# An expert's last rows as one step of 32, 64 or 96 rows: the expert loop of a graph network with a mixture of experts

## The chip, the cores and the metric

The kernel runs on one core of a Trainium2 chip. The metric is device time in microseconds, the median of several runs. The profile beside it is one execution of the same program, taken by the hardware profiler; its span runs from the first instruction to the last.

## The reference

The input is a graph of 625 nodes with 768 features each and 20,000 edges. Two layers of graph attention come first, then a transformer block whose feed-forward part is a mixture of eight experts, all in float32. Every node goes to the one expert with the largest gate value (`K = 1`, so its weight is 1):

```python
gate_logits = h2 @ Wg                                   # h2: 625 x 768, Wg: 768 x 8
w, sel = jax.lax.top_k(gate_logits, 1)
hid = relu(einsum('nd,edf->enf', h2, W1) + b1)          # W1: 8 x 768 x 3072
y = einsum('enf,efd->end', hid, W2) + b2                # W2: 8 x 3072 x 768
out = x + einsum('ne,end->nd', combine, y)              # combine: one 1 in each row
```

The reference computes every expert for every node and keeps one. The kernel computes each node's own expert alone. How many nodes an expert gets is known only when the gate has run.

## The kernel before, in words

**Before the experts.** The graph layers and the attention take the first 640 us. As each block of 125 nodes leaves the attention, `gate` and `choose` find its experts, and `send` scatters its rows into two DRAM buffers, `xg` (what the expert reads) and `xr` (what the result is added to), sorted by expert: an expert has 640 places (`RE`).

**The first expert.** The expert that most nodes of the first block chose is loaded early; up to 128 of its rows are worked on as `step_a` while the last blocks are still being sent.

**The step table.** Meanwhile VectorE works out, on one partition, what is left to do (L1194 to L1294). It sorts the experts by size, splits each one's rows into steps and fills a table with one column for each step: expert, whether its weights are new, kind of step (0: 128 rows, 1: 64, 2: 32) and first row. An expert's rows are rounded up to a multiple of 32; the multiple of 128 in them gives steps of 128, and what is left (0, 32, 64 or 96) a step of 32, one of 64, or one of each. Within an expert the step of 32 comes first, then that of 64, then those of 128. The table has room for `NS` = 20 steps; the intermediate arrays have 20 x 8 = 160 elements.

**The loop over steps** (L1321 to L1340). In each turn GpSimd gathers the next step's rows into `xb` (L1328) and this step's sums so far into `rb` (L1046); then `tc.If` chooses one of three bodies, `step(128)`, `step(64)` or `step(32)`. The code of each body stands in the program once on every engine.

**A step of M rows** has P = 128 / M groups. The stationary operand of a matmul is then only M columns wide, and P of them stand side by side in the tensor engine and in PSUM, each with another slice of the weights. W1 and W2 each lie in SBUF in three pieces of 3 MB (`w1[c]`, `w2[c]`), each loaded in two halves. A step of 32 or 64 rows takes a piece at a time:

- `into(c)` (L1074): rows times piece c of W1 into the PSUM tile `ph`, and VectorE copies that to `hb` (L1083).
- `turn(c)` (L1086): TensorE turns `hb` (L1090); ScalarE adds the bias, takes the ReLU and writes `hbT` (L1095).
- `out_of(c)` (L1097): `hbT` times piece c of W2, summed over all c in the PSUM tile `py` (L1102).

The order on TensorE is written out (L1130 to L1141): all `into` with the `turn`s between them, then all `out_of`; among the last two of these the next step's rows are turned (`turn_rows`, L879). At the end VectorE adds `py`, group by group, to `yo`, which holds the sums so far and the bias `b2` (L1149 to L1154), and GpSimd scatters `yo` to the output (L1156).

**The weights.** There is one set of buffers. After each step's code SyncE has `load_expert` (L1054) for the next step: six halves of W1 (L1025), the bias block `b2b` (L1031), six halves of W2 (L1019). Each is issued when the current step no longer reads what it overwrites. All issues carry a condition: where the next step has the same expert, they are passed over and no byte is moved.

## Time and profile before

| | |
|---|---|
| median of 3 runs | 1089.4 us (1086.68 to 1089.96) |
| the profiled execution: time | 1088.95 us |
| its span | 1086.4 us |
| PE busy | 1012.5 us, 93% of the span |
| VectorE, ScalarE, GpSimd busy | 450.8, 318.8, 57.9 us |
| mean granted TensorE clock | 0.978 |
| `step_a` on PE | from 642.3 |
| nine steps of the loop on PE | 714.5 to 1073.7 |

The page names engines PE (matmuls), PEld (weight loads into the array, beside PE), DVE (VectorE), ACT (ScalarE), POOL (GpSimd) and SP (SyncE); a q behind the name is the engine's sequencer, which waits, branches and issues transfers. "L1102" is a line of the kernel. A float32 matmul of the program shows as two records. In a group's line the bar is followed by its busy time, the mean ns of one, and the idle time of the engine before it with what ended that. The chain of waits follows the work back from the last instruction, at each step to what released it.

PE's share of 93% is a mean over stages with different limits: the attention and the graph layers are not touched by this change, and in the loop the share differs from step to step.

### The profile page before, as it was taken

What the parts mean: (1) busy time and instruction counts of PE and PEld (TensorE: products, weight loads), DVE (VectorE), ACT (ScalarE), POOL (GpSimd) and SP (SyncE); (2) the same over time, 40 slices, a digit from 0 to 9 for tenths busy, and PEclk for the clock granted to TensorE, in tenths of its full rate; (3) what the DMA queues carried; (4) which work ended last, traced back from release to release, by engine and by line L of the source; (5) the groups of instructions that cost most, each with busy time, mean ns of one, the idle gap of its engine ahead of it and who ended that gap; (6) DMA issues with size and microseconds to landing.
All of it is one profiled execution on the core that took longest, in us unless ns stands there. A gap on an engine that the chain in (4) does not pass through costs nothing. (4 is left out here: it accounts for less than half of the span.)

```text
span 1086.4 us, 14453 instructions
## 1 busy us (share of the span) xinstructions
PE 1012.5 (93%) x4763; PEld 578.2 (53%) x4764; DVE 450.8 (41%) x1264; ACT 318.8 (29%) x820; POOL 57.9 (5%) x97
## 2 busy tenths in 40 slices
PE   6889799999989989999999999999999889998993
PEld 4455366677555556666765655544454435533341
DVE  6796776385174740465546655011101121011211
ACT  6677534362140020344443401110201112021120
POOL 1200100000000100000000111000000000000000
PEclk9999899999999999999999999999999899998997
DMA  9300400300430164999200759111799948899694
GB/s 287 121 1 1 157 1 0 131 1 19 102 97 1 51 125 80 404 377 342 76 1 3 288 176 373 59 46 37 274 325 381 403 179 325 297 406 403 244 405 159
DMA packets 85669, 194.48 MB, mean 179 GB/s; under 512 B 32397, under 2 KB 34068, under 8 KB 85609
## 3 DMA queue, kind: packets, MB, share of 16 engines
q1 hardware_dynamic: 79817, 174.00, 44.9%
q0 software_dynamic: 5712, 19.54, 5.1%
q8 instruction: 36, 0.59, 0.2%
q10 hardware_dynamic: 80, 0.16, 0.1%
q14 instruction: 24, 0.20, 0.1%
HBM read 251.98 MB, written 38.37 MB: 267 GB/s over the span
## 5 line engine op out<-in xcount | busy, mean ns | idle before, releaser
L1102 PE MATMUL py<-ew,hbT 128*64 128x384 f32 (+2 forms) x960 | 194.4, 512 | 16.2 <-DMA ew<-in_L_ffn_W_dram 16.0
L1079 PE MATMUL ph<-ew,xbT 128*32 128x256 f32 (+2 forms) x864 | 155.6, 501 | 8.4 <-issue 4.8
L1102 PEld LDWEIGHTS py<-ew,hbT 128*64 128x64 f32 (+2 forms) x960 | 91.3, 149 | 101.0 <-issue 65.5
L1095 ACT ACTIVATE hbT<-tph,bT 128x64 f32<-128x64 f32 (+2 forms) x240 | 55.4, 333 | 267.4 <-PE tph L1090 166.2
L1079 PEld LDWEIGHTS ph<-ew,xbT 128*32 128x32 f32 (+2 forms) x864 | 64.8, 136 | 88.6 <-issue 81.7
L1154 DVE TENSOR_TENSOR yo<-yo,py 64x384 f32<-64x384 f32 (+2 forms) x40 | 23.0, 608 | 184.3 <-PE py L1102 183.9
L1083 DVE COPY hb<-ph 128x512 f32<-128x512 f32 (+1 forms) x39 | 24.4, 629 | 152.1 <-PE ph L1079 152.1
L515 PE MATMUL agg<-xl,zT 125*125 125x256 f32 (+1 forms) x300 | 79.8, 417 | 1.4 <-ACT zT L504 1.3
L515 PEld LDWEIGHTS agg<-xl,zT 125*125 125x125 f32 x300 | 54.5, 188 | 19.7 <-ACT zT L504 2.8
L227 ACT ACTIVATE step<-iota,past 125x314 f16<-125x314 f16 x120 | 55.9, 549 | 0.0
L352 PE MATMUL pp<-w,yT 128*125 128x512 f32 x120 | 55.3, 600 | 0.0
L613 PE MATMUL ph<-wr,h1T 128*125 128x384 f32 x160 | 54.5, 498 | 0.0
L577 PE MATMUL ph<-w,h1T 128*125 128x384 f32 x160 | 52.4, 486 | 0.0
L162 PE MATMUL ph<-wr,yT 128*125 128x512 f32 x96 | 44.4, 621 | 5.9 <-DVEq L445 5.9
L825 ACT ACTIVATE e<-e,nm 125x125 f32<-125x125 f32 (+4 forms) x60 | 36.0, 602 | 39.3 <-DVE nm L822 39.3
L244 PE MATMUL cps<-step,oh 125*125 125x314 f16 x181 | 37.1, 307 | 10.5 <-ACT step L227 7.4
L888 PE MATMUL po<-wpj,aT 128*125 128x384 f32 x120 | 44.3, 499 | 1.2 <-DVE nm L822 0.7
L237 DVE TENSOR_SCALAR oh<-iota,drel,upper 125x125 f16<-125x125 f16 x160 | 41.0, 313 | 3.2 <-PE cps L244 3.1
L613 PEld LDWEIGHTS ph<-wr,h1T 128*125 128x125 f32 x160 | 30.6, 193 | 21.6 <-issue 1.7
L577 PEld LDWEIGHTS ph<-w,h1T 128*125 128x125 f32 x160 | 30.0, 188 | 21.1 <-issue 0.5
L796 PE MATMUL pq<-hT,L_ffn_Wq 128*128 128x313 f32 (+1 forms) x144 | 41.0, 432 | 0.0
L822 DVE CUSTOM_DVE_ANT_0 e<-sc,later 125x125 f32<-125x125 f32 (+4 forms) x60 | 30.7, 543 | 24.0 <-PE sc L816 23.8
(326 smaller groups left out, 1252.3 us busy)
## 6 DMA issues: line engine op xcount, KB each, us to landing
ew<-in_L_ffn_W_dram SPq DMA_DIRECT2D x132, 1536.0 KB
xr<-zt SPq DMA_DIRECT2D x5, 3076.0 KB
xg<-zt SPq DMA_DIRECT2D x5, 3072.0 KB
w<-in_L_gnn_W_dram SPq DMA_DIRECT2D x4, 1536.0 KB
wr<-in_L_gnn_Wr_dram SPq DMA_DIRECT2D x4, 1536.0 KB
b2b<-in_L_ffn_b_dram SPq DMA_DIRECT2D x11, 384.0 KB
xb<-xg POOLq DMA_DIRECT2D x10, 384.0 KB, 6.4
rb<-xr POOLq DMA_DIRECT2D x9, 384.5 KB, 7.1
```

The lines of the kernel that those rows point to most:

```text
L162: nc.tensor.matmul(pp[:R, :], yT[:, c, cols(t)], part(wr1, KD, c, i, 512), start=(c == 0), stop=(c == KD - 1))
L227: nc.scalar.activation(o, iota[:, :SH + 1], AF.Sign, bias=at, scale=-1.0)
L237: m = nc.vector.tensor_scalar(o, iota[:, :n], at, weight, op0=OP.is_equal, op1=OP.mult)
L352: nc.tensor.matmul(pp[:R, :], yT[:, c, cols(t)], part(w1, KD, c, i, 512), start=(c == 0), stop=(c == KD - 1))
L515: nc.tensor.matmul(self.agg[:R, c0:c0 + n], zT[:, s, :], xl[:, s, x0:x0 + n], start=(s == 0), stop=(s == T - 1))
L577: nc.tensor.matmul(ph[:R, :384], h1T[:, c, cols(t)], part(w2, KH, c, i, 384), start=(c == 0), stop=(c == KH - 1))
L613: nc.tensor.matmul(ph[:R, :384], h1T[:, k, cols(t)], part(wr2, KH, k, i, 384), start=(k == 0), stop=(k == KH - 1))
L796: nc.tensor.matmul(pp[:, :b - a], w[:, c, c0:c0 + 128], hT[:, c, a:b], start=(c == 0), stop=(c == KD - 1))
L888: mm = nc.tensor.matmul(pp[:R, i, :384], aT[:, c, cols(t)], wpj[i][:, c, :], start=(c == 0), stop=(c == KD - 1))
L1079: mm = nc.tensor.matmul(ph[g * M:(g + 1) * M, :C], xT[:, k, :M], w[:, k, o + g * C:o + (g + 1) * C], start=(k == 0), stop=(k == KD - 1))
L1095: nc.scalar.activation(hbT[c][:, k, r], tp[:, k, r], AF.Relu, bias=bT[:, f:f + 1])
L1102: mm = nc.tensor.matmul(py[g * M:(g + 1) * M, i, :384], hbT[c][:, k, g * M:(g + 1) * M], w[:, o + g * K + k, i * 384:(i + 1) * 384], start ...
```

## The change

An expert's last rows (32, 64 or 96) become one step. There is a fourth kind of step, of 96 rows, in place of a step of 32 followed by one of 64. It is worked as two parts, `subs`: 64 rows with P = 2 and 32 rows with P = 4. Each piece of W1 and W2 is used for the 64 rows and then for the 32, so the list of items is (piece 0, 64), (piece 0, 32), (piece 1, 64) and so on, six in all, and `into`, `turn` and `out_of` take an item where they took a piece. The 32 rows sum in a second `py` tile, from a PSUM pool `second`, which is opened in the place of the routing's pool once that is closed; to that end the pool `sp` is now opened before the routing's `ps`. An expert's steps come in the order: the part first, then those of 128. The table's part of the code is shorter, and `NS` is 13 instead of 20. The loop that adds `py` to `yo` has a new width: for the single sizes it is half of what it was, so a step has eight adds instead of four; a step of 96 has four of 64 rows and four of 32 rows with the widths as before.

The core of the diff:

```diff
-NS = E * 2 + N // B
+NS = E + N // B + 1
...
-    ps = ctx.enter_context(tc.tile_pool(name="rps", bufs=1, space=PSUM, reuse_waits="tile"))
     sp = ctx.enter_context(tc.tile_pool(name="sps", bufs=2, space=PSUM, reuse_waits="tile"))
+    routing = ctx.enter_context(ExitStack())
+    ps = routing.enter_context(tc.tile_pool(name="rps", bufs=1, space=PSUM, reuse_waits="tile"))
...
+        subs = []
+        for m, o in ((64, 0), (32, 64)) if M == 96 else ((M, 0),):
+            P = B // m
+            C = 512 if P == 1 else FC // P
+            where = sp if not o else second
+            subs.append((m, o, P, C, where.tile([128, 2, 512], F32, name="py", bufs=1)))
+        m, _, P, C, _ = subs[0]
+        last_c = DF // (C * P) - 1
+        items = [(c, *sub) for c in range(last_c + 1) for sub in subs]
+        n = len(items)
...
-                    mm = nc.tensor.matmul(ph[g * M:(g + 1) * M, :C], xT[:, k, :M],
+                    mm = nc.tensor.matmul(ph[g * m:(g + 1) * m, :C], xT[:, k, r0:r0 + m],
...
-        for g in range(P):
-            for cc in range(4 // P):
-                w = 384 * P // 4
-                cs = slice(cc * w, (cc + 1) * w)
-                nc.vector.tensor_add(yv[:, :, cs], yv[:, :, cs], py[g * M:(g + 1) * M, :, cs])
+        for m, r0, P, _, py in subs:
+            yv = yo.rearrange("p (i c) -> p i c", i=2)[r0:r0 + m]
+            w = 384 * len(subs) * P // 8
+            for g in range(P):
+                for cc in range(384 // w):
+                    cs = slice(cc * w, (cc + 1) * w)
+                    nc.vector.tensor_add(yv[:, :, cs], yv[:, :, cs], py[g * m:(g + 1) * m, :, cs])
...
+    v.tensor_max(size, n64, n32)
+    v.scalar_tensor_tensor(part_kind, n32, 2.0, n64, op0=OP.mult, op1=OP.add)
...
+    routing.close()
+    second = ctx.enter_context(tc.tile_pool(name="sqs", bufs=1, space=PSUM, reuse_waits="tile"))
...
-                all_of(step(32, xbT, bT, rb, first_turned), *then)
+                with tc.If(kind == 2) as cmp3:
+                    all_of(step(32, xbT, bT, rb, first_turned), *then)
+                with cmp3.Else():
+                    all_of(step(96, xbT, bT, rb, first_turned), *then)
```

In the table, behind the gathered fields, fourteen operations on all columns give way to six; before them, on the eight experts, two give way to six.

## The prediction

> **What bounds the kernel now.** I read the page first, for the shares of the engines and the costliest groups; then the tensor engine's order of time, to find the steps of the expert loop; then SyncE's weight transfers; then the chain that ended last, for the waits between steps. All times are us from the start of the profiled span of 1086.4.

> In the time order of the tensor engine the loop shows as nine steps of 64, 128, 64, 32, 128, 64, 32, 64 and 32 rows, numbered 1 to 9 here. One row of the stretches each for steps 6 to 9 (columns: stretch, its length, busy time and count on PE, PEld, DVE, ACT, POOL, granted clock, DMA share, GB/s):

> ```profile
> 948.50:982.70 34.20, 34.20 (x189) 13.47 (x188) 4.32 (x10) 6.08 (x26) 2.12 (x3) 1.00 0.99 389
> 982.70:1011.30 28.60, 21.98 (x254) 9.63 (x252) 4.58 (x10) 5.44 (x26) 2.06 (x3) 0.88 0.88 343
> 1011.30:1045.50 34.20, 34.20 (x188) 13.52 (x186) 6.96 (x10) 6.08 (x26) 2.00 (x3) 1.00 0.84 329
> 1045.50:1073.80 28.30, 21.70 (x254) 9.45 (x252) 4.60 (x11) 5.44 (x26) 2.04 (x3) 0.94 0.89 348
> ```

> A step of 64 rows keeps PE busy without a hole; steps 7 and 9, of 32 rows, have holes. SyncE tells whose weights each step has (start, length, number of issues; L1025 loads the W1 pieces, L1019 the W2 pieces):

> ```profile
> 952.79 12.59 SPq L1025 DMA_DIRECT2D ew<-in_L_ffn_W_dram  x6
> ...
> 970.90 21.98 SPq L1019 DMA_DIRECT2D ew<-in_L_ffn_W_dram  x6
> 996.88 12.22 SPq L1025 DMA_DIRECT2D ew<-in_L_ffn_W_dram  x6
> ...
> 1009.87 2.71 SPq L1019 DMA_DIRECT2D ew<-in_L_ffn_W_dram  x6
> 1016.11 12.13 SPq L1025 DMA_DIRECT2D ew<-in_L_ffn_W_dram  x6
> ...
> 1033.77 22.07 SPq L1019 DMA_DIRECT2D ew<-in_L_ffn_W_dram  x6
> ```

> The set issued in step 7 (996.88 and 1009.87) moves nothing: its W2 issues pass in 2.71 where a real set takes 22, and in the stretch after it the DMA rate is 0 (below). So step 8 uses step 7's weights: steps 7 and 8 are the 32 and the 64 rows of one expert, in the table's order (32 before 64 before 128). Skipped sets also stand before steps 1, 2 and 5; the other pairs on one expert are therefore 64+128 and 32+128. **Steps 7 and 8 are the only pair that the change makes one.** What the chain of waits says about them:

> ```profile
> 982.76 4.48 PE ph L1079 x80
> ...
> 987.34 21.12 DMA ew<-in_L_ffn_W_dram
> ...
> 1008.60 2.77 PE py L1102 x28
> 1011.37 10.45 PE ph L1079 x48
> ...
> 1050.02 20.81 DMA ew<-in_L_ffn_W_dram
> ...
> 1070.96 2.80 PE py L1102 x28
> ```

> Step 7 waits for the end of its expert's load (last piece at 1008.46). Then step 8 runs from loaded weights, while the last expert's load (for step 9) has only begun at 1016.11, because the single set of buffers is in use. Step 9 then waits until 1070.82. In these stretches the DMA stands idle for 7.6 and then runs at its ceiling:

> ```profile
> 965.00:1008.50 43.50, 36.98 (x334) 16.43 (x332) 6.12 (x13) 9.78 (x44) 2.06 (x3) 0.92 0.99 391
> 1008.50:1016.10 7.60, 7.50 (x52) 2.76 (x54) 3.97 (x5) 0.00 (x0) 0.00 (x0) 1.00 0.00 0
> 1016.10:1028.00 11.90, 11.90 (x59) 4.11 (x56) 1.60 (x3) 1.75 (x8) 2.00 (x3) 1.00 0.91 344
> 1028.00:1070.80 42.80, 36.43 (x333) 16.09 (x331) 5.98 (x13) 9.78 (x44) 2.04 (x3) 0.96 1.01 397
> ```

> **Term 1, the joined step: -10.7.** PE work of one step of 96: a 64 part without its turning of the next rows, 34.2 - 0.8 = 33.4, and a 32 part, which without waits is 5.3 for two `into`, 2.7 for the third and for each `out_of`, and 0.37 for each of three turns: 17.2. With the 0.8 for the turning of the next rows back it is 51.4, against 62.8 for steps 7 and 8 now; of the 11.4 saved 10.5 are DMA wait, not arithmetic. Placed at 982.7, its six `into` and five turns end at 1009, just as the last W2 piece lands (1008.46), so it never waits for its own weights. It gives its first W1 piece free after two `into` (990.7), the third at 1008.6, the W2 pieces at 1017.5, 1025.6 and 1034. SyncE reaches this set at 996.9, as now, but now it is the last expert's real load. It queues behind the W2 pieces in flight, and DMA goes on without the idle stretch at 1008.5 and without the slow one after it. Its bytes are 12 pieces of 1536 KB, the bias row block of 384 KB, one pair of gathers (768 KB; the other pair goes with the iteration) and a scatter of 288 KB: 20.3 MB, at 391 to 397 GB/s 51.3 to 52. It lands at about 1060.1, against 1070.82. A half piece takes 3.9 at that rate, so the transfers come to the third W1 piece at 1024, to the three W2 pieces at 1033, 1041 and 1048: each release is at least 14 ahead. PE alone could end step 9 at 1034.1 + 18.1 = 1052; after the last half piece it needs 2.8, as now, so the end is 1063 and the weights are still what is late.

> The new body must be fetched when it runs first. The row is the first run of 32 rows in step 4: PE idle 4.8, then 6.8 at a granted clock of 0.50, some 2.2 lost; 7.0 in all. This stands between 0 (if the code lies in what was fetched already, since the new body follows that of 32) and 7.0. I take 7.0: PE alone could then end at 1059 instead of 1052, still before 1063, and the releases are still 7 ahead: it costs nothing. Without that cover it would be 7.0 on the path.

> Tile widths change within a step now: 64 to 32 columns, three times with no turn between. Rows: four turns take 0.44 in a step of 128 and 0.59 in one of 64, so two changes of width cost 0.15; three more cost 0.2, under the same cover. [...]

> The second PSUM tile takes the banks that the routing gives back at about 662, 320 before its first use: 0; at the front the pools change places, which can move the first expert's first `into`, now held 0.5 by DVE, by +-0.5. ACT does 16 short activations per pair of items (5.1) beside 9 of PE: 0.

> **Term 2, the smaller table: -1.2.** PE stands 1.68 before 674.39, waiting for an `hb` copy that queues on DVE behind the table (662.2 to 673.7). Thirteen operations on 160 elements (0.31 each; 64 elements took 0.21) go to 104, say 0.25: -0.8. Behind the last reduction (ends 671.8) the final cast began 1.7 later; four dependent operations at 0.2 are left before it: -0.9. Ahead, four more on eight elements, partly side by side: +0.5. From here to step 4 PE has hardly a hole, so it shifts all that follows. Bounds: 0 and -1.68.

> **Term 3, the last sums: +0.3.** The widths in the loop over `py` are halved for the single sizes, so a step has 8 adds, not 4. Four adds of 384 per partition went from 748.87 to 750.95, so eight are 4.2; the four of 768 that end the kernel took 3.9. The one place inside where PE waited for these sums is the start of step 2 (2.3, until 751.09; the sums ended at 750.95): eight adds of 192 at the 0.27 from start to start of the first step's take 2.1, the four now 2.1: 0. The fourth branch costs each engine one compare (0.1 to 0.2), hidden except in steps of 32.

> **Sum:** the profiled execution took 1088.95; -10.7 - 1.2 + 0.3 = -11.6 gives 1077.35. The median of the three runs is 0.45 above it, so 1077.8.

> **Rivals.** *B, code fetched anew.* The weights set the end only if PE begins step 9 by about 1045. After the long new body, loop head or 32-row body may have to be fetched once more. The row:

> ```profile
> L1337 PEldq COMPARE_BRANCH  x11: 72/191/6041, 713.5 to 1044.0; - x11
> ```

> A branch to code at hand takes 0.2; the worst took 6.04, before step 4. From step 5 on none is long, though all three bodies alternate. One such miss (6.0 less the 3.2 that PE's sequencer runs ahead, and 2.2 of clock) added to 1059 ends PE at 1064, 1 late; a second puts it at 1072, 9 late: 1079 to 1087.

> *C, slower.* The same mechanism at every boundary. The loop holds 2 x (186 + 198 + 252) = 1272 matmuls and weight loads now and 2 x 432 = 864 more after (64 and 32 rows, less one turning of the next rows, 6). If that no longer stays on the engine, steps 5 and 6, which are bound by PE, each pay 7.0 as step 4 did, on top of the 9 at the end: 1077.8 + 23 = 1101. It decides from two such misses on the path (the sum is worth 11.6). For it: two exits (745 and 849) missed while the loop was young. Against it: until step 7 the new body isn't run, and what steps 5 and 6 need is what they need now. [...]

> *D, nothing is joined,* or the load is not brought forward: 1088 to 1089. The skipped set in step 7 speaks against it.

> **Chances.** A, as summed, 0.57 (own range 1075 to 1081: terms 2 and the DMA rate); B 0.23; C 0.13; D 0.07. The 8-in-10 range reaches over A and B: 1074 to 1088. Under 0.3% (3.3 us) a measurement of this kernel can't be told from no change; so faster 0.79 (A, and B but for its end), within 0.3% 0.08 (D, the end of B), slower 0.13 (C).

> **What would show it.** Eight steps, the seventh of 96 rows with PE busy for some 51; no DMA stretch at 0 GB/s between the last two loads; the last wait for weights ending near 1059; PE's hole before 674.39 down to 0.5; eight sums at the end. Long branches on PE before steps 5, 6 or 8 would mean B or C; a last step that waits for PE and not for weights, B.

## The result, and the profile after

| | before | after |
|---|---|---|
| median | 1089.45 us (1086.68 to 1093.41, 12 runs) | 1088.98 us (1087.02 to 1091.74, 12 runs) |
| ratio, 95% interval | | 0.9994 (0.9980 to 1.0008) |
| span of the profiled execution | 1086.4 us | 1087.7 us |
| PE ends at | 1073.73 | 1074.85 |

No change that can be measured: 1077.8 was forecast. Yet the trace after shows nearly all that the change was to bring. The tensor engine's order of time has eight steps: 64, 128, 64, 32, 128, 64, 96 and 32 rows. One row for steps 6, 7, the stretch behind it, and step 8 (columns as before: stretch, length, busy time and count on PE, PEld, DVE, ACT, POOL, granted clock, DMA share, GB/s):

```profile
950.90:985.05 34.15, 34.15 (x188) 13.65 (x189) 4.58 (x14) 6.08 (x26) 2.12 (x3) 1.00 1.00 391
985.05:1037.05 52.00, 52.00 (x434) 21.14 (x430) 8.81 (x21) 10.79 (x50) 2.06 (x3) 1.00 1.03 404
1037.05:1049.41 12.36, 0.01 (x1) 0.03 (x1) 3.98 (x5) 0.00 (x0) 2.07 (x3) 0.68 1.03 398
1049.41:1074.90 25.49, 21.04 (x252) 9.05 (x252) 2.19 (x5) 5.44 (x26) 0.00 (x0) 0.82 0.45 172
```

The joined step keeps PE busy for 52.0 without a hole, and DMA runs through it at a share of 1.03 and 404 GB/s. But then PE does nothing for 12.36, and the last step takes 25.5 instead of some 18. SyncE's loads of the last two weight sets:

```profile
955.26 12.57 SPq L1025 DMA_DIRECT2D ew<-in_L_ffn_W_dram  x6
...
973.36 22.46 SPq L1019 DMA_DIRECT2D ew<-in_L_ffn_W_dram  x6
1000.03 17.49 SPq L1025 DMA_DIRECT2D ew<-in_L_ffn_W_dram  x6
...
1021.56 23.47 SPq L1019 DMA_DIRECT2D ew<-in_L_ffn_W_dram  x6
```

The skipped set of 2.71 is gone, and the last expert's set starts in step 7. Its last bytes arrive between 1061 and 1062:

```profile
1061.00:1062.00 1.00, 1.00 (x18) 0.37 (x10) 0.00 (x0) 0.00 (x0) 0.00 (x0) 1.00 0.16 61
1062.00:1063.00 1.00, 1.00 (x16) 0.60 (x18) 0.42 (x1) 0.38 (x3) 0.00 (x0) 1.00 0.00 0
```

The last landing is at 1062.57, that is 77.5 after step 7 began; before it was 88.1 (1070.82). So the weights came 10.6 earlier, and the time did not follow. (An expectation below has 1060.5 for this landing, which is too early.) The chain of waits tells what is late instead:

```profile
1022.96 20.75 DMA ew<-in_L_ffn_W_dram
1043.71 5.71 issue
1049.41 1.03 PE ph L1087 x3
1050.45 4.39 issue
1054.84 7.21 PE ph L1087 x93
```

"issue" means that PE waited for nothing that the profile shows. No later piece of weights stands in the chain: behind 1054.84 all is PE, to its end. The branches of PE's sequencer give the reason (columns: minimum, median and maximum in ns; first and last start). L1344 is the test for 128 rows, L1347 that for 64, L1350 that for 32:

```profile
L1344 PEldq COMPARE_BRANCH  x10: 88/222/6735, 712.6 to 1036.3; - x10
L1347 PEldq COMPARE_BRANCH  x9: 72/207/6001, 716.0 to 1043.1; - x9
L1350 PEldq COMPARE_BRANCH  x5: 72/337/4475, 857.3 to 1072.7; - x5
```

After the body of 96 the sequencer, 0.7 ahead of PE, goes on to the body of 32: the test at the loop's head takes 6.74 (from 1036.33), the next 5.79 (from 1043.12), and after three matmuls of the new body there is another stop of 4.39. The instruction queue tells the same (columns: packets, MB, share). In the whole execution it moves 50 packets of 16 KB, before the change 36. From step 5 to the end of step 6 it moves none. Then come four in the joined step, three in the stop of 12.36, one from the start of the last step to the end of its stop of 4.39, and four behind that; the lines show the whole and then these four stretches:

```profile
q8 instruction: 50, 0.82, 0.3%
...
q8 instruction: 4, 0.07, 0.5%
q8 instruction: 3, 0.05, 1.9%
q8 instruction: 1, 0.02, 1.2%
q8 instruction: 4, 0.07, 1.8%
```

Before the change the queue moved eleven packets from 709.97 to 870.00, where each of the three bodies ran for the first time, and none from step 5 to PE's end.

### The profile page after: what moved, and what is told of

Read it like the earlier page. It is cut to its first block, busy times and chain, and to the rows that moved or that the text cites. A ratio compares the mean times of both kernels' runs of the same rounds, so it can differ in the third digit from the quotient of the medians.

```text
span 1087.7 us, 14317 instructions
## 1 busy us (share of the span) xinstructions
PE 1009.8 (93%) x4757; PEld 577.2 (53%) x4758; DVE 450.9 (41%) x1289; ACT 318.4 (29%) x818; POOL 55.1 (5%) x94
## 5 line engine op out<-in xcount | busy, mean ns | idle before, releaser
L1114 PE MATMUL py<-ew,hbT 128*64 128x384 f32 (+2 forms) x960 | 188.3, 495 | 4.1 <-DMA ew<-in_L_ffn_W_dram 4.1
L1087 PE MATMUL ph<-ew,xbT 128*32 128x256 f32 (+2 forms) x864 | 156.3, 506 | 25.5 <-issue 21.7
L1167 DVE TENSOR_TENSOR yo<-yo,py 128x96 f32<-128x96 f32 (+4 forms) x72 | 25.2, 403 | 173.2 <-PE py L1114 172.8
L244 PE MATMUL cps<-step,oh 125*125 125x314 f16 x181 | 37.3, 310 | 10.5 <-ACT step L227 5.4
L759 PE MATMUL pv<-L_ffn_Wv,hT 128*125 128x384 f32 x120 | 41.3, 502 | 0.0
```

The source lines that it names most:

```text
L759: nc.tensor.matmul(pp[:R, :384], hT[:, c, cols(t)], w[i][:, c, :], start=(c == 0), stop=(c == KD - 1))
L1087: mm = nc.tensor.matmul(ph[g * m:(g + 1) * m, :C], xT[:, k, r0:r0 + m], w[:, k, o + g * C:o + (g + 1) * C], start=(k == 0), stop=(k == KD ...
L1114: mm = nc.tensor.matmul(py[g * m:(g + 1) * m, i, :384], hbT[j][:, k, g * m:(g + 1) * m], w[:, o + g * K + k, i * 384:(i + 1) * 384], start ...
```

## The experiments

Ten kernels. "PE's code of the loop" is the number of instructions from the loop's head to its end on PE's sequencer, counted in the built programs (to within two; no trace shows it): 1402 before, 2311 after. The theory to be tested (1): the body of 96 pushes the other bodies' code out, and it has to be brought back on the way to the last step. Its rival (2): the joined step itself makes PE wait, by its second sum tile, its gathers or its doubled sums. And a third (3): it is the loop's length in memory, whether the new body runs or not.

**as128: the joined step without a new body.** Two operations in the table of the kernel before:

```diff
-    v.tensor_scalar(n128, units, 0.25, -0.375, op0=OP.mult, op1=OP.add)
+    v.tensor_scalar(n128, units, 0.25, -0.125, op0=OP.mult, op1=OP.add)
...
+    v.tensor_scalar(rest, rest, 0.0, None, op0=OP.max)
```

> The kernel before with one change in its table: 96 rows left become a step of 128 (two table operations differ), so steps 7 and 8 are one step without any new body; the three bodies, their code, the sums and the larger table stay as they were. The step is 65.4 of PE work (the row of step 5) instead of 62.8 with waits, but it takes one set of weights over its whole length, so the last set of weights starts as early as in the changed kernel. Theory 1 (the joined step is worth what was forecast, the new code took it away): no long branch from step 7 on, the last load lands near 1060, PE ends the joined step at about 1048 and the last at 1066: 7.7 less than 1073.7, time 1081.5 (1079.5 to 1083). Theory 2 (joining brings nothing, whatever the body): 1089 to 1092.

Measured: 1079.57 us (1077.86 to 1084.82), ratio 0.9912 (0.9885 to 0.9939). Joined step and last step in its profile:

```profile
980.90:1046.25 65.35, 65.35 (x201) 34.74 (x199) 7.29 (x13) 7.80 (x26) 2.06 (x3) 1.00 1.03 405
1046.25:1064.45 18.20, 18.18 (x253) 8.52 (x252) 3.69 (x10) 5.44 (x26) 2.13 (x3) 1.00 0.52 202
```

The joined step is 13.35 longer on PE than that of 96 rows, and still the two steps end 83.5 after the start of the first, against 89.8 in the changed kernel and 91.0 before. The last step begins the moment the joined one ends, and PE is busy throughout. No branch from step 5 on is long (the longest of the whole loop are 3.7 and 3.2):

```profile
L1335 PEldq COMPARE_BRANCH  x11: 78/201/3712, 712.5 to 1042.3; - x11
...
L1338 PEldq COMPARE_BRANCH  x8: 72/192/3234, 716.2 to 1042.6; - x8
```

So a join without new code brings its gain: 7.5 from step 7 to PE's end, where 7.7 had been expected for this wider step. From `step_a` to PE's end this execution saves 11.5 in all; the other 4.0 lie ahead of step 5, where the execution before had a granted clock of 0.86 in the first `into` of step 2 and the stop before the first step of 32 rows. It doesn't yet tell theory 1 from 2, since the second sum tile is gone as well.

**no32: the body of 96 as it is, another body left out.**

```diff
-                with tc.If(kind == 2) as cmp3:
-                    all_of(step(32, xbT, bT, rb, first_turned), *then)
-                with cmp3.Else():
-                    all_of(step(96, xbT, bT, rb, first_turned), *then)
+                all_of(step(96, xbT, bT, rb, first_turned), *then)
```

with `part_kind` = `n32` + `n64`.

> The changed kernel without the body of 32: 32 rows left are worked by the body of 64 (steps 4 and 8), the body of 96 is as in the changed kernel, with its two sum tiles, its gathers and its eight sums. PE's code of the loop is 1766 instructions. Theory 1 (code): no idle time of 12 us between the step of 96 and the last; the last step is 34.2 on PE instead of 18 and starts where that of 96 ends, step 4 becomes some 1 to 3 longer: PE ends at 1073 to 1077, time 1086 to 1092. Theory 2 (the 12 us belong to the step of 96 itself, to its data or its sums): the idle time stays, 1098 to 1104.

Measured: 1094.20 us (1093.11 to 1095.70), ratio 1.0051 (1.0031 to 1.0071). The last `into` of the joined step and the first of the last step, in PE's order of time (start, length):

```profile
1015.18 2.80 PE L1087 MATMUL ph<-ew,xbT 128*32 128x256 f32 x48
...
1043.92 10.52 PE L1087 MATMUL ph<-ew,xbT 128*64 128x512 f32 x48
```

The line has no idle time before it, and the joined step takes 51.96 (991.96 to 1043.92): the body of 96, with both sum tiles, ends without any wait behind it. Theory 2 falls. The row says more: here too the body of 96 (904 instructions) has just run, and the way from the loop's head is free. So it is not the length of that body alone that makes the stops. That the kernel is slower is the price of 32 rows in a body of 64: 34.3 instead of 18.2 at the end, and 35.7 instead of 27.8 from the start of step 4 to that of step 5 (I had put the latter at 1 to 3 more, it is 7.9, so the time lies above the 1086 to 1092 expected).

**dead96: the body of 96 in the program, never run.** The changed kernel with the step table of before, so nine steps.

```diff
-NS = E + N // B + 1
+NS = E * 2 + N // B
...
-    for i, a in enumerate((base, part_kind, part_rows, number, done)):
+    for i, a in enumerate((base, n32, n64, number, done)):
```

> The changed kernel with the step table of before: the body of 96 stands in the code behind that of 32 and is never run; nine steps, as before. Theory 1 (what is run is what fills the fetched code): no long branch before steps 5 to 9, time as before, 1089 (1086 to 1092, the leaving of the 32 body may cost 3 once where it has a label and a jump more). Theory 3 (the loop's length in memory alone is what costs, the misses come at the distance): long branches before the last steps as in the changed kernel, 1095 to 1105.

Measured: one run, 1093.50 us; before on the same chip 1090.69 (up to 1092.23). This time lies between the two expectations and decides nothing; the branches do. No branch is long behind step 4:

```profile
L1349 PEldq COMPARE_BRANCH  x11: 83/214/3653, 713.1 to 1048.0; - x11
L1352 PEldq COMPARE_BRANCH  x11: 72/194/5981, 716.8 to 1048.3; - x11
L1355 PEldq COMPARE_BRANCH  x6: 72/129/3452, 858.2 to 1075.9; - x6
```

The 5.98 is at 850.28, on the way to the first step of 32 rows, as before the change; the 3.45 at 881.62 is the leaving of that body, and it is new: in the changed kernel it stands at 880.56 with 3.18. Theory 3 falls: a body that only lies in memory causes none of the three stops. But the end of the body of 32, which was followed by the loop's end, now needs a jump over the body of 96. Whether dead code costs a little time, one run can't show.

**copy128, only64, short1, short2: how much code.** Four lengths of the fourth body. copy128: a second copy of `step(B)` in the place of `step(96)`. only64, short1 and short2 leave out rows' work, as their expectations say:

```diff
-        for m, o in ((64, 0), (32, 64)) if M == 96 else ((M, 0),):
+        for m, o in ((64 if M == 96 else M, 0),):
...
-        items = [(c, *sub) for c in range(last_c + 1) for sub in subs]
+        items = [(c, *sub) for c in range(last_c + 1) for sub in subs if not sub[1] or c < 1]
```

(the first is only64, the second short1; short2 has `c < 2`; in both the end of the 32 rows' sum moves to the last piece used).

> The changed kernel with another fourth body: 96 rows left are worked by a second copy of the body of 128 rows, so that there are four bodies, but PE's code of the loop is 1840 instructions and not 2311, and the fourth body is 435 and not 904. Theory 1a (the length of the code that is run decides): none or one long branch after the fourth body has run, time 1079 to 1083, like e4_as128 plus at most a fetch of the new body and 3 for leaving a body. Theory 1b (any fourth body pushes the others out): two or three long branches before the last step, as in the changed kernel, and 8 to 14 more: 1088 to 1094.

> The changed kernel whose fourth body works only the first 64 of the 96 rows (the experts' output for the last 32 rows of that step is left out; everything around it stays). PE's code of the loop is 1817 instructions, and the last step is reached over the same two labels as in the changed kernel. Theory 1a (length): no long branch before the last step, which waits for its weights: they land near 1060, PE ends at 1063 to 1066, time 1077 to 1081. Theory 1b (a fourth body or the walk over two labels as such): two long branches before the last step; PE then has done its 33 us by 1019 and the branches lie under the wait for the weights, so the time stays at 1077 to 1081 and only the branches tell.

> The changed kernel whose fourth body works the 64 rows in full and the 32 rows with the first piece of W1 and W2 only (two thirds of the experts' output for those 32 rows are left out). PE's code of the loop is 1978 instructions. [...] Theory 1d (the longer, the more is lost, without an edge between): one long branch of about 6 before the last step already.

> As e8_short1, with two of the three pieces for the 32 rows (a third of their output is left out). PE's code of the loop is 2145 instructions. [...]

| kernel | PE's code of the loop | long branches between joined and last step | PE idle for them before the last step, and in its first `into` | packets of the instruction queue in the joined step, and from there to PE's end | time, us |
|---|---|---|---|---|---|
| as128 | 1402 | none | 0 | 0, 0 | 1079.57 |
| no32 | 1766 | none | 0 | 3, 0 | 1094.20 |
| only64 | 1817 | none | 0 | 0, 0 | 1078.95, one run |
| copy128 | 1840 | none | 0 | 0, 0 | 1084.76 (1078.90 to 1086.33) |
| short1 | 1978 | 6.64, 5.91 | 11.18 + 4.22 | 3, 6 | 1085.46, one run |
| short2 | 2145 | 6.70, 5.91 | 11.15 + 4.39 | 3, 8 | 1085.86, one run |
| changed | 2311 | 6.74, 5.79 | 12.36 + 4.39 | 4, 8 | 1088.98 |

The branches and stops are those of one execution of each kernel. The times come from several chips (before, beside them: 1090.69, 1089.20 and, for short1 and short2, one run of 1092.52).

The rows that carry it, in PE's order of time: the start of the last step in short1,

```profile
1036.33 1.03 PE L1087 MATMUL ph<-ew,xbT 128*32 128x256 f32 x3 [11.18 <-issue]
1041.58 6.97 PE L1087 MATMUL ph<-ew,xbT 128*32 128x256 f32 x93 [4.22 <-issue]
```

and in copy128:

```profile
1050.53 5.39 PE L1087 MATMUL ph<-ew,xbT 128*32 128x256 f32 x96
1056.21 2.80 PE L1087 MATMUL ph<-ew,xbT 128*32 128x256 f32 x48
```

It looks like an edge and not a slope: up to 1840 instructions PE stands idle for no branch behind the joined step, from 1978 on the same three stops appear. The packets say the same: up to 1840 the queue moves none from the joined step's end to PE's end, also in no32, where three come in during the joined step; from 1978 on it moves six to eight. I had expected short1 to be free, and it was not. What sets the edge, and where between 1840 and 1978 it lies, no run shows.

only64 also shows where the weights would end the kernel: its last piece lands 76.1 after step 7's start, PE ends 81.6 after it, 5.35 for the last 28 matmuls at a granted clock of 0.50. copy128 lies above as128 by its median, but the ratios 0.9941 (0.9917 to 0.9964) and 0.9912 (0.9885 to 0.9939) overlap.

**32first and 32last: other orders of the same code.** 32first has the bodies in the order 32, 64, 128, 96:

```diff
-        with tc.If(kind == 0) as cmp:
-            all_of(step(B, xbT, bT, rb, first_turned), *then)
+        with tc.If(kind == 2) as cmp:
+            all_of(step(32, xbT, bT, rb, first_turned), *then)
...
-                with tc.If(kind == 2) as cmp3:
-                    all_of(step(32, xbT, bT, rb, first_turned), *then)
+                with tc.If(kind == 0) as cmp3:
+                    all_of(step(B, xbT, bT, rb, first_turned), *then)
```

> The order of the bodies in the code is changed and nothing else: 32, 64, 128, 96 in the place of 128, 64, 32, 96; every step does the same work in the same order. Theory 1 (code): the last step lost 12.36 + 4.39 us in the changed kernel because PE walked from the loop's head over two labels to the body of 32, and each was fetched anew at 5.8 to 6.7 us. Here the body of 32 stands right behind the loop's head, so at most one fetch is left: the last step waits for its weights (last piece landed at 1060.5 in the changed kernel), PE ends at 1063 to 1067 instead of 1074.85, time 1078 to 1083. Theory 2 (a wait in the data: the second sum tile, the doubled adds, the gathers): nothing moves, 1089, and the same 12 us of idle time stand before the last step. In the other steps a branch may turn long that was short, since body 64 and 128 are now walked to over other labels; each such miss on the path would cost 3 to 7.

Measured: 1107.93 us (1099.94 to 1111.75), ratio 1.0139 (1.0098 to 1.0181). Where I had looked, it was right: the last step (from 1077.00) begins without a stop and loses 0.90 in it. But three other steps now begin late, the second, third and sixth, and the joined step after them by 5.04 (a branch of 6.02 ends 0.33 before it; the view itself puts this wait to the weights):

```profile
762.10 13.41 PE L1087 MATMUL ph<-ew,xbT 128*128 128x512 f32 x24 [11.53 <-issue]
...
841.00 13.18 PE L1087 MATMUL ph<-ew,xbT 128*64 128x512 f32 x48 [10.63 <-issue]
...
981.02 13.14 PE L1087 MATMUL ph<-ew,xbT 128*64 128x512 f32 x48 [10.99 <-issue]
```

Before the third and the sixth the sequencer shows three long branches in a row: out of the body of 128 (4.03, 3.85), back to the loop's head (4.13, 4.37), on from the head (6.40, 6.70). The 13.1 to 13.4 are an `into` that took 10.57 (128 rows, from 883.09) and 10.52 (64 rows, from 948.44) in the execution before, at a granted clock of 1.00.

> The kinds are numbered anew (0: 128, 1: 64, 2: 96, 3: 32; one table operation on eight elements more) and the bodies stand as 128, 64, 96, 32; the body of 32 is reached from the loop's head by one branch and lies behind that of 96. Work as in the changed kernel. Theory 1 (code): one branch to the body of 32 instead of two labels, and its code was fetched ahead behind that of 96 or has to be fetched once: at most 6 to 7 us before the last step instead of 12.36, and no second stop: time 1078 to 1084. Theory 2 (a wait in the data): 1089 and 12 us before the last step, as in the changed kernel.

32last was built with the bodies as 128, 32, 64, 96, not in the order that the expectation gives. (The order is read from the built program. The trace bears it out in part: L1345, the test for 32, shows ten branches, eight tests and two jumps out of the body of 32, so that body isn't the last.) Measured: 1088.89 us (1084.67 to 1093.58), ratio 0.9988 (0.9970 to 1.0005). Out of the sixth step, of 64 rows, it had a long branch of 6.05, then 5.57 back to the head; PE stood idle for 10.25 before the joined step. Before the last step it had one of 6.35 and 6.00 of idle time. From the joined step's start PE needed only 81.1 to its end; the gain went ahead of it. Neither order brings the gain back: moving the code moves the stops.

**three: the changed kernel with three bodies.** Its table, pools and sums, but 96 rows as a step of 128 (two table operations more):

```diff
-                with tc.If(kind == 2) as cmp3:
-                    all_of(step(32, xbT, bT, rb, first_turned), *then)
-                with cmp3.Else():
-                    all_of(step(96, xbT, bT, rb, first_turned), *then)
+                all_of(step(32, xbT, bT, rb, first_turned), *then)
```

> The changed kernel (its shorter table, its pools, its eight sums) with three bodies only: 96 rows left are a step of 128 rows, as in e4_as128. PE's code of the loop is 1402 instructions, as before, in the place of 2311. Theory 1 (the new body's code took the gain): as e4_as128 measured (1079.6, 0.991 of before), less 1.4 for the table and plus 0.3 for the sums: 1078.5 (1076 to 1081), no long branch on PE from step 7 on, PE's hole ahead of the second turn at 0.3. Rival (the sums, the pools or the table cost what the join brought): 1083 or more, and the loss shows in those stretches.

Measured: 1081.51 us (1078.57 to 1084.14), ratio 0.9923 (0.9905 to 0.9941): faster than both kernels, and not to be told from as128. The joined and the last step end after 83.5, as in as128; PE's hole ahead of the second turn is 0.35. Its shorter table is seen there, but not in the time of the whole.

## Why the prediction was wrong, by its own steps

**The failed step is in term 1: the code that has to be fetched again after the long body stands in it at nothing.** The sum counts one fetch, the new body's own (7.0, under the cover of the weights). That no other would come was the condition of the 0.57, and it failed. What the runs showed in its place: three stops. The sequencer's lead was 0.7 and counted once for both labels (6.74 and 5.79), so they cost 12.36, in which three packets of the instruction queue came in; the stop in the body 4.39; and the last step's 25.44 less this stop is 2.95 more than the 18.1 forecast for it (as128 has 18.20 at a granted clock of 1.00), while the granted clock was 0.50 to 0.74 until 1062. That is 19.7 on a PE path of 52.0 + 18.1 = 70.1 behind step 7's start. The weights, as only64 shows them, would have ended it at 81.6 (its granted clock of 0.50 at the end included). So the cover was 11.5, of which the prediction knew (it had PE alone end 4 to 11 before the weights), and 19.7 - 11.5 = 8.2 came out on top: 89.8, as measured. From the start of step 7 to PE's end it was 91.0 before: 1.2 was left of the 10.7.

**Rival B had the mechanism, and part of its number by luck.** Its sign, a last step that waits for PE and not for weights, is what the trace shows. Its case of two misses ends PE at 1072, which is 89.3 behind step 7's start, against 89.8 measured. But it got there with 7.0 for the new body's first fetch, which cost nothing, and 13 for two misses, where three stops cost 19.7. The prediction had given it 0.23.

**The evidence was read too far.** "From step 5 on none is long, though all three bodies alternate" shows a loop of 1402 instructions whose branches stay short there (none above 0.25); it says nothing of 2311. The prediction held the count (1272 matmuls and weight loads and 864 more) and put it under C. Against a loss it set one argument, which meets C only: what steps 5 and 6 need is what they need now. That was right: from step 5 to the end of step 6 the instruction queue moves no packet. But the last step comes after the new body.

**Term 1, its other parts.** The joined step: 52.0, forecast 51.4. The last weights: 77.5 after step 7's start, forecast 77.4 (1060.1 less 982.7). The end of the idle DMA stretch: as forecast. The new body's own first fetch: 0 of 7.0; four packets come in during the joined step, but PE goes from step 6 to step 7 without a hole and through step 7 without one, and in copy128 and only64 the fourth body runs for the first time without a packet. The row behind the 7.0 was no first fetch of a body either: the branch of 6.04 at 849.06 is the jump out of the body of 64 rows, and the test that leads into the body of 32 took 0.21 there. The join's worth where no code is fetched: 7.5 in as128's tail, whose step is 13.35 longer. The full 10.7 no kernel shows; only64, which leaves out a part of the work, comes to 91.0 - 81.6 = 9.4.

**Not foreseen: the leaving of the body of 32.** The prediction had one compare of 0.1 to 0.2 for the fourth branch. The jump over the new body took 3.18 at 880.56, but PE was busy all that time; it shows only as a hole of 0.66 before step 5. (The view puts the hole to a sum of VectorE's, but in four kernels with this jump and such a hole, the changed one, copy128, short1 and short2, step 5 begins 1.83 to 1.84 after the jump's end.) From step 3 to step 5 the changed kernel needs 67.15, before 64.98. Of these 2.2 more, 1.3 are the last piece of step 4's weights, for which PE waits until 880.44, 62.0 behind step 3's start; before it was 60.7. Why it comes later is open; it is not the jump, since three, which has no jump there, needs 66.87.

**Term 2, the table: right.** -1.4, forecast -1.2; the hole is now

```profile
676.99 0.66 PE L1100 MATMUL tph<-ident,hb 128*128 128x128 f32 x4 [0.30 <-DVE hb L1091]
```

and from `step_a`'s first `into` to step 1's it is 72.15 before and 70.72 after. **Term 3, the last sums: right.** 3.90 before, forecast +0.3:

```profile
1074.99 4.17 DVE L1167 TENSOR_TENSOR yo<-yo,py 32x384 f32<-32x384 f32 x8 [8.36 <-PE py L1114]
```

**The sum** of the two executions, from `step_a`'s first `into` to PE's end: -1.4 (table), -2.3 in steps 1 and 2 (1.7 of it in the first `into` of step 2: 12.23 at a granted clock of 0.86 before, 10.54 at 1.00 after), +2.2 (steps 3 and 4), -0.1, -1.2 (the tail): -2.9, 431.4 to 428.5. The front took 4.0 more in the execution after, with the same work on PE. Over the kernels here `step_a` starts between 640.5 and 646.3, so of the medians 0.5 and the single execution's 2.9 are not at odds.

**What stays open.** What decides which branches turn long is not settled. The edge between 1840 and 1978 holds for this order of bodies and steps; in 32first, with the changed kernel's bodies in another order, branches of 3.85 to 6.70 stood already behind the run of one body of 64 or of 128 rows (435 instructions). And as128, whose code and path up to step 6 are those of before, had no long branch on the way to the first step of 32 where before had one of 6.04 and three, with a loop as long, one of 5.96.

## What to carry to other kernels

A new body in a loop over steps can cost more than the time that it runs: what comes after it may have to be fetched again, here at 6.74 and 5.79 us for the two labels on the way, at a DMA share of 1.03. So count the loop's instructions on the engine that has most of them, before and after, and look whether the profile has long branches already. A gain made under a cover must be reckoned against everything that uses up the same cover. If the same regrouping can be had by sending the work through a body that exists, even a wider one (65.4 against 52.0 here, where the last weights were late enough to cover most of the difference), try that first.

## What the runs showed of the hardware

```profile
709.97:713.35 3.38, 3.15 (x10) 1.52 (x8) 0.19 (x1) 0.00 (x0) 0.00 (x0) 1.00 0.02 5
745.42:749.16 3.74, 3.37 (x22) 1.28 (x18) 0.29 (x1) 0.00 (x0) 0.00 (x0) 1.00 0.02 4
849.06:855.10 6.04, 3.37 (x22) 1.28 (x18) 2.04 (x4) 0.00 (x0) 0.00 (x0) 0.97 1.02 399
```

At a DMA share of 0.02 they took 3.38 and 3.74, and PE's queued matmuls hid 3.15 and 3.37 of that. With the weights moving (1.02) it was 6.04, and 2.67 showed; with the walk to the body behind it PE stood for 4.79. Of the two in a row in the changed kernel nothing of the second was hidden (5.79). In the loops of all twelve kernels here the long branches took 3.2 to 3.9 at a DMA share of 0.03 or less, and 5.6 to 6.7 at 0.98 or more; two at the end of the last step took 4.4 to 4.5 at 0.05 or less, and in both the instruction queue moved two packets. Between these shares they took 3.9 to 6.7. No run changes the DMA load alone, so that it is the cause is not shown.

- Behind the stops the granted clock was low: 0.50, then 0.74 up to 1062.05. The last step of the changed kernel, stretch by stretch:

```profile
1049.41:1050.45 1.04, 1.03 (x3) 0.16 (x3) 0.00 (x0) 0.00 (x0) 0.00 (x0) 0.50 1.03 405
1050.45:1054.84 4.39, 0.00 (x1) 0.00 (x1) 0.00 (x0) 0.00 (x0) 0.00 (x0) 0.50 1.02 394
1054.84:1062.05 7.21, 7.21 (x94) 3.45 (x95) 0.42 (x1) 0.00 (x0) 0.00 (x0) 0.74 0.78 302
1062.05:1074.90 12.85, 12.79 (x157) 5.44 (x156) 1.76 (x4) 5.44 (x26) 0.00 (x0) 1.00 0.02 4
```

The work behind the stops of 12.36 and 4.39 thus took 2.95 more than the forecast 18.1.
